# Five lanes instead of six in a four-block transformer stack: slots, banks, pairs and a new order of work

## The chip, the cores and the metric

The kernel runs on one core of one Trainium2 chip. The metric is the device time of one execution in microseconds (us), as the median of several runs; lower is better. A profile is one execution of its own, recorded by the hardware profiler. In it PE is TensorE (matrix products), PEld its loading of weights, DVE is VectorE, ACT is ScalarE, POOL is GpSimd and SP is SyncE, which issues nearly all transfers (DMAs) here.

## What is computed

Thirty-two sequences of 64 tokens with 256 features, all in float32, pass through four blocks one after the other. `ctx` has the same shape and stays as it is.

```python
def stack(x, ctx):                       # both (32, 64, 256)
    x = block0(x, ctx)   # 16 heads of 16; queries from x, keys and values from concat(ctx, x): 128 a sequence
                         # masked softmax, out_w, + x, rmsnorm, gelu(. @ w1) @ w2 (1024 wide), + x
    x = block1(x, ctx)   # layernorm, token shift, five mixes, then a recurrence over the 64 tokens
                         # with a state of 32 heads x 8 x 8, whose start is rows 2..9 of ctx;
                         # group norm, gate, Wo; then a channel mix with fWk, fWr, fWv
    x = block2(x, ctx)   # layernorm, self attention (q, k, v = three parts of w_qkv), layernorm,
                         # cross attention over ctx, layernorm, gelu(. @ w1 + b1) @ w2, each + x
    x = block3(x, ctx)   # cross attention over layernorm(ctx), x + tanh(gate) * out
    return x
```

In the recurrence each head holds a state `s` of 8 x 8; for each token `out = r . (faaaa * k v + s)` and `s = k v + w * s`.

## The kernel before, in words

**Groups, jobs and lanes.** The sequences form NG = 8 groups of GB = 4, so a group is 256 tokens, held as 128 partitions by two tiles of 256 features (token major) or as two chunks of 128 features by 256 tokens (feature major). One block of one group is a job: 32 jobs. A *lane* (class `Lane`, line 388) is a private set of buffers in which one job runs at a time: `SLOTS` slots in SBUF of 2080 bytes a partition (`L.s()`, `L.d()`), a few small tiles, and `BANKS` PSUM banks of 128x512. There are NL = 6 lanes of 10 slots; lanes 0 and 1 have two banks, the other four have one, eight in all. All lanes share the engines.

**The list of jobs.** `JOBS` (line 59) names, in the order in which lanes become free, the block of the next job; `next_job` (1536) gives it the first group that is ready for that block. Each block is a Python generator, and the loop from line 1574 advances the lanes in turn, one `yield` each. Groups pass `x` from one block to the next through DRAM (`load_x`, `store_x`).

**The order of the instructions.** What the loop records is not the order that runs. `order_instructions` (378) takes the recorded instructions, works out what each depends on, and `list_schedule` (283) puts them into one order with a cost of each from `Op.cost` (157): of those that could start, the earliest goes first, and among equals the one of lowest rank. The rank is the place at recording plus an entry of `PUT_BACK` (90), one entry for each RUN = 30 instructions. Each engine then executes its own instructions strictly in that order, and waits on semaphores where it must.

**Products.** `matmul` (516) has two forms. With plain float32 operands it is one instruction (line 520). With *pairs* each operand is a float32r high part and a float32r rest, and the product is three float32r instructions (line 523): high by high, high by rest, rest by high. `split` (509) makes a pair from an activation: a ScalarE copy (512) and a VectorE subtraction (513). `load_w` (501) makes one from a weight: a transfer into a staging buffer, of which there is one (`STAGES`), a ScalarE copy (505) and a VectorE subtraction (506); a pair of weights takes two of the `W_BUFS` = 27 weight buffers, a plain weight one. `SPLIT` says which blocks use pairs: before, blocks 0 and 3. Block 2's cross keys and values are pairs in any case. A projection of one group (`project_T`, 618, or `project`, 632) is four products of 128x256 for each 256 columns of weight, into one bank. In block 2 `SPLIT` decides over q, k and v (lines 1389, 1390, 1399) and the four parts of w1 (1414), and over the split of what the first and the third layernorm give (1450, 1476).

**Attention.** Scores are taken by a quarter of the heads at a time (`r` = 0 to 3), in matmuls of 64 rows by 64 columns of the array: `attention64` (774) for blocks 2 and 3, line 787, and line 987 for block 0; line 888 lays a mask under them where there is one. Below, one `r` is called a head. `side_by_side` (763) takes two such heads at once, on different halves of the array's rows, in lanes with more than one bank, and one at a time in the others. Then `softmax_unit` (731) finds the maximum on VectorE (736), subtracts it (738), transposes on TensorE (744), and exponentiates on ScalarE (745). In block 2 the scores are first masked by VectorE (1438) and GpSimd (1439). Sums over keys (800, 999) and products with the values (810, 1013) use columns of 32.

**Block 1.** The recurrence runs along the tokens by VectorE's scan (1293), 128 scans of 260 columns, between products on VectorE (1290, 1297); line 1303 sums over the state's rows on TensorE. Each job of it makes 16 transfers of 128 KB each from `vd` in DRAM.

**Two places that the change touches besides.** `weights1` puts the initial state of the recurrence into place (lines 1111 to 1125): four transfers of rows of ctx into the staging buffer, and for each eight matmuls with the identity (line 1120), whose weights are every eighth column of the rows, into a bank of lane 0. And block 0 starts by loading ctx and x tiles (line 907), all on SP's queue; the first such pair is lane 0's, group 0, tile 0, transposed by TensorE at line 911. ScalarE's queue issues the constants at the start (539 to 549).

Of the kernel before, what the change touches and what calls it, by code (L numbers as in the profile page):

```python
# [44 lines left out]
P = 128  # L45
B, S, D = 32, 64, 256
NC = D // P
GB = 4
NG = B // GB
W_BUFS = 27  # L50
STAGES = 1
NL = 6
SLOTS = (10, 10, 10, 10, 10, 10)
STAGGER = 4

SPLIT = (0,3)
BANKS = (2, 2, 1, 1, 1, 1)

JOBS = "00010110000111222211233222333333"
GT = GB * S  # L60
TT = GT // P
NH, DH = 16, 16
# [3 lines left out]
HS = 8  # L66
# [21 lines left out]

RUN = 30
PUT_BACK = (  # L90
    -151, -197, 167, -46, 45, -228, -363, -247, 293, 104, -401, -687, -701, -257, -2, 122, -362,
    -546, -151, -305, -598, -113, -406, -253, 285, 87, 144, -352, 182, 97, -397, 471, 223, -176,
    -102, -136, -405, 153, -17, -213, 335, -950, -802, -808, -81, -197, -36, -73, -62, -390, -287,
    -198, -344, -179, 96, 109, -55, -46, 76, 31, -186, 136, -193, 388, -122, -155, -25, -49, 84,
    -346, -135, -279, -555, -592, -190, 1, 46, 55, -5, 34, 220, -102, 175, 263, 161, 365, 177, 333,
    315, 92, 40, 382, 320, 472, 316, 52, -349, -11, -488, -32, -197, -653, -428, -646, -112, -21,
    104, -11, 323, 14, -30, 59, -342, -206, -1207, -1842, -47, -62, -77, -410, 107, 66, 49, 245,
    -243, 50, 105, -347, -77, -279, -21, -179, -201, -751, -308, -188, 134, -60, 2, -472, -574, 174,
    54, -91, -79, -201, 139, -81, -37, 116, -329, 40, -21, -186, 234, 134, 243, 209, -112, -48, 95,
    319, 36, -120, 40, 91, 53, 125, 66, 184, 215, -383, 105, 280, -80, 40, -108, 230, 77, 67, -36,  # L100
    153, 378, -26, 267, 539, 363, 360, 540, -223, 603, -972, -232, -692, 173, 77, 168, -418, -345,
    0, -69, -1239, -1027, -382, -58, -41, 50, -626, 123, 106, -244, 162, -304, 121, 484, 398, 1009,
    438, 401, 299, -29, -187, -274, -49, -69, -90, 65, -55, 280, 46, 837, 722, 85, 335, -61, -90,
    94, -634, 189, -1199, -486, -41, -21, -173, -217, -199, 223, -202, -131, -59, 287, 395, 467,
    423, -358, 136, -59, 32, -226, 109, 72, -389, -543, 228, 248, 513, 404, 120, 266, 46, -340, 312,
    506, -835, -53, 144, -152, 89, -55, 348, 746, 370, -67, -146, 272, -234, -198, 20, 215, 603,
    -20, 161, 1029, 1278, -429, -199, -75, 292, 91, 256, -46, 196, 6, 139, 252, 17, -214, -417, -63,
    -115, -193, -223, -263, -199, 23, 1083, 252, 416, 768, 675, -48, -156, 83, 352, 1157, 140, 134,
    177, 281,
)  # L110
ENGINES = ("PE", "DVE", "Activation", "Pool", "SP")
LATENCY = {"PE": 40, "DVE": 34, "Activation": 33, "Pool": 34}
# [6 lines left out]
class Op:  # L119
# [37 lines left out]
    def cost(self, n, psum, wide):  # L157
        ins, kind = self.ins, self.kind
        self.lock, self.load, self.table = False, 0.0, None
        if kind == "DMACopy":  # L160
            self.ns, steps = 400.0, ins.outs[0].ap
            self.bytes = 4
            for _, m in steps:
                self.bytes *= m
            if len(steps) > 2:
                self.ns = 480.0
        elif self.engine == "PE":
            moving, weights = ins.ins[0], ins.ins[1]
            dt = str(moving.dtype).split(".")[-1]
            cols = 1  # L170
            for _, m in list(moving.ap)[1:]:
                cols *= m
            m = 1
            for _, k in list(weights.ap)[1:]:
                m *= k
            passes = {"float32": 4, "float32r": 1}.get(dt, 1)
            if ins.is_transpose:
                passes = 2
            self.ns = passes * cols / 2.4 + {4: 4, 2: 2}.get(passes, 9 if dt == "float32r" else 2)
            self.load = m * {"float32": 0.6, "float32r": 0.3}.get(dt, 0.2) / (2 if ins.is_transpose else 1)  # L180
            (r, c), (h, w) = ins.tile_position, ins.tile_size
            self.shape = (h, w)
            self.cells = [
                (i, j) for i in range(r // 32, (r + h + 31) // 32) for j in range(c // 32, (c + w) // 32)
            ]
        elif self.engine == "DVE":
            self.ns = {
                "BNStats": 415, "BNStatsAggregate": 165, "StreamTranspose": 190 + 1.02 * n,
                "Reciprocal": 130 + 6.7 * n, "TensorCopy": 80 + n, "TensorReduce": 62 + 1.2 * n,
            }.get(kind, 62 + 1.21 * n)  # L190
            if kind == "TensorTensor":
                self.lock = wide > 1
            elif kind == "TensorScalarPtr":
                if ins.is_tensor_tensor_scan:
                    self.ns, self.lock = 670.0, True
                elif ins.is_scalar_tensor_tensor:
                    self.ns, self.lock = 210 + 1.04 * n, wide > 1
                else:
                    self.ns, self.lock = 140 + 0.95 * n, not psum
        elif self.engine == "Activation":  # L200
            func = str(getattr(ins, "func", "")).split(".")[-1]
            self.table = TABLES.get(func)
            if func == "Exp" and n >= 512:
                self.ns = 597.0
            elif kind == "TensorCopy":
                self.ns = (364.0 if n <= 256 else 590.0) if psum else 100 + 1.02 * n
            else:
                self.ns = 400.0 if n <= 128 else 470.0 if "Gelu" in func else 560.0 if n <= 256 else 680.0
        else:
            self.lock = kind not in ("Memset", "RegisterMove")  # L210
            if kind == "TensorTensor":
                self.ns = 703.0 if n <= 2 else 60 + 2.41 * n
                self.lock = n > 2
            else:
                self.ns = {"Memset": 95 + 0.84 * n, "TensorCopy": 190 + 0.5 * n}.get(kind, 190 + 0.84 * n)
# [209 lines left out]
def kernel(ctx: ExitStack, tc: tile.TileContext, a: dict, out: bass.AP):  # L425
    nc = tc.nc
# [473 lines left out]
    def block0(L, g):  # L900
        mb = key_mask(L, "mask0", g, mybir.dt.int32, 2 * S)
        ct = None
        for i in range(TT):

            cl = tok2(L.d())
            for h, src in enumerate((a["ctx"], a["x"])):
                nc.sync.dma_start(out=cl[:, h], in_=token_major(src, g)[:, i, :])
            ps = L.bank("T").rearrange("p (c h t) -> p c h t", c=NC, h=2)
            for c in range(NC):
                for h in range(2):  # L910
# [152 lines left out]
    def weights1():  # L1063
# [47 lines left out]
        for h in range(2):  # L1111
            ps = lanes[0].bank("T")[:, : NC * HS * B // 2].rearrange("p (t b) -> p t b", b=B)
            for u in range(2):
                st_rows = mk(wpool, [P, NC, D], "stage", STAGES).rearrange("p c n -> p (c n)")
                nc.sync.dma_start(
                    out=st_rows[:B],
                    in_=a["ctx"][:, 2 + 4 * h + 2 * u : 4 + 4 * h + 2 * u, :].rearrange("b s d -> b (s d)"),
                )
                for t in range(HS):
                    nc.tensor.matmul(  # L1120
                        ps[64 * u : 64 * u + 64, t, :],
                        lhsT=st_rows[:B, t : t + (P // 2 - 1) * HS + 1 : HS], rhs=ident[:B, :B],
                        start=True, stop=True,
                    )
            nc.vector.tensor_copy(s0T[:, h], ps)
# [261 lines left out]
    def weights2():  # L1387
        yield
        W["l2_q"] = wload(2, "l2_wqkv")
        W["l2_k"] = wload(2, "l2_wqkv", col0=D)  # L1390
        W["kb2"] = masked_bias("l2_kb", ind)
        W["qb2"] = masked_bias("l2_qb", par)
        W["m1"] = mk(const, [P, S], "m1")
        for j in range(2):
            nc.sync.dma_start(out=W["m1"][j * S : (j + 1) * S, :], in_=a["mask1"][0, 0])
        W["f1"] = mk(const, [P, S], "f1")
        mask_fill(W["f1"], W["m1"])
        yield
        W["l2_v"] = wload(2, "l2_wqkv", col0=2 * D)
        load_row("l2_aob", rows_d)  # L1400
        W["cqb2"] = masked_bias("l2_cqb", par)
        W["ckb2"] = masked_bias("l2_ckb", ind)
        yield
        W["l2_ao"] = mload("o", "l2_wao")
        W["l2_cq"] = mload("c", "l2_wq")
        yield 0
        W["l2_ck"] = load_w("l2_wkv")
        yield 0
        W["l2_cv"] = load_w("l2_wkv", col0=D)
        load_row("l2_cob", rows_d)  # L1410
        load_row("l2_b2")
        W["l2_co"] = mload("o", "l2_wco")
        yield 0
        W["l2_w1"] = [wload(2, "l2_w1", col0=o) for o in range(0, DFF, D)]
        yield 0
        W["l2_w2"] = [mload("h", "l2_w2", row0=o) for o in range(0, DFF, D)]
# [292 lines left out]
```

## Time and profile before

| what | value |
|---|---|
| runs | 1040.76, 1044.8, 1045.53 us; median 1044.8 |
| the profiled execution | 1046.34 us, of which the span from first to last instruction is 1044.6 us |
| mean granted TensorE clock | 0.985 |
| instructions in the trace | 25099 |
| TensorE busy, first 26 us | 17.29 us |
| TensorE busy, 26 to 52 us | 24.90 us |
| TensorE busy, each 100 us from 200 to 1000 | 95.7, 98.6, 96.8, 91.6, 98.3, 100.0, 98.4, 98.3 us |
| TensorE busy, last 45 us | 40.15 us |
| VectorE busy, the same eight stretches | 81.3, 71.7, 88.8, 79.9, 88.0, 64.1, 79.4, 42.3 us |
| HBM traffic over the span | 64 GB/s |

A line of the page's groups reads: source line, engine, operation, output from inputs by tile name, shapes, how many; then busy time in us and the mean of one in ns; then how long the engine stood idle just before them, and what ended that. A float32 product shows as two records, a float32r product or a transpose as one. Records of TensorE overlap their neighbours, so the time that a matmul takes from the stream is read from the distance between starts, in the chain of work or in the timeline.

### The profile page before, as it was taken

The numbers are of one execution on the slowest core, as the hardware profiler recorded it, in microseconds if no ns is written. First come the engines' busy times: TensorE is split into PE (matmuls) and PEld (weight loads), VectorE is DVE, ScalarE is ACT, GpSimd is POOL, SyncE is SP. The second block draws the span as 40 slices with busy tenths as digits, with TensorE's granted clock in tenths as the row PEclk, the third lists the DMA queues.
The fourth block names the chain that finished last, engine by engine and source line by source line (L and its number), as shares of the span: only waits on it lengthen the run. The fifth ranks groups of instructions, "written<-read, shape, count | busy, mean of one in ns | idle before, by whom it ended". The sixth has DMA issues, their size and how long they took to land. (4 is left out here: it accounts for less than half of the span.)

```text
span 1044.6 us, 25099 instructions
## 1 busy us (share of the span) xinstructions
PE 1006.0 (96%) x10012; PEld 826.2 (79%) x10012; DVE 739.1 (71%) x1446; ACT 608.9 (58%) x1241; POOL 350.9 (34%) x501
## 2 busy tenths in 40 slices
PE   6999999999999999999889999999999999999998
PEld 5778878867897786888667878887888788878886
DVE  4662466988867758889878788889655779672157
ACT  6657435454584575546636746565877665654471
POOL 1111033115322414553534665333334543432000
PEclk9999999989999999999969999999999999999999
DMA  6711132411321233233141202222021110010101
GB/s 182 209 36 45 56 94 84 148 52 58 119 65 55 64 101 107 77 102 101 41 132 52 77 24 68 80 71 84 2 82 52 32 42 23 11 42 31 42 21 42
DMA packets 81204, 73.34 MB, mean 70 GB/s; under 512 B 11882, under 2 KB 76864, under 8 KB 81088
## 3 DMA queue, kind: packets, MB, share of 16 engines
q1 hardware_dynamic: 80140, 71.69, 22.4%
q8 instruction: 79, 1.29, 0.5%
q14 instruction: 37, 0.30, 0.1%
q10 hardware_dynamic: 948, 0.05, 0.1%
HBM read 51.77 MB, written 14.68 MB: 64 GB/s over the span
## 5 line engine op out<-in xcount | busy, mean ns | idle before, releaser
L520 PE MATMUL bank<-w,s 128*128 128x256 f32 x1024 | 242.7, 384 | 1.2 <-POOL s L1350 0.6
L520 PEld LDWEIGHTS bank<-w,s 128*128 128x128 f32 x1024 | 190.2, 191 | 30.9 <-issue 2.7
L520 PE MATMUL bank<-s,w 128*128 128x256 f32 x832 | 205.2, 386 | 2.7 <-ACT s L612 2.4
L520 PEld LDWEIGHTS bank<-s,w 128*128 128x128 f32 x832 | 150.5, 191 | 31.1 <-ACT s L612 6.1
L745 ACT ACTIVATE s<-bank 128x512 f32<-128x512 f32 x160 | 92.7, 599 | 102.7 <-PE bank L744 72.2
L523 PE MATMUL bank<-s,w 128*128 128x256 f32 x768 | 120.9, 299 | 0.3
L1439 POOL TENSOR_TENSOR s<-s,f 128x512 f32<-128x512 f32 x64 | 85.5, 1347 | 90.6 <-DVE s L1438 90.4
L523 PEld LDWEIGHTS bank<-s,w 128*128 128x128 f32 x768 | 101.2, 190 | 7.4 <-ACT s L939 1.4
L744 PE MATMUL bank<-ident,s 128*128 128x128 f32 x640 | 97.6, 281 | 5.8 <-DVE s L738 4.6
L744 PEld LDWEIGHTS bank<-ident,s 128*128 128x128 f32 x640 | 74.8, 143 | 25.2 <-issue 12.2
L736 DVE TENSOR_REDUCE mx<-bank 128x4 f32<-128x512 f32 (+1 forms) x96 | 63.7, 681 | 42.1 <-PE bank L987 23.1
L1293 DVE TENSOR_TENSOR_SCAN s<-s,s 128x260 f32<-128x260 f32 x128 | 89.0, 723 | 0.4
L825 ACT ACTIVATE s<-bank,vecs 128x256 f32<-128x256 f32 x128 | 53.4, 470 | 47.5 <-PE bank L520 23.9
L787 PE MATMUL bank<-s,s 64*64 64x128 f32 x1536 | 75.0, 276 | 1.0 <-ACT s L745 0.9
L787 PEld LDWEIGHTS bank<-s,s 64*64 64x64 f32 x1536 | 63.4, 134 | 14.8 <-issue 6.5
L605 ACT ACTIVATE s<-s,shift,rstd 128x256 f32<-128x256 f32 x96 | 52.3, 595 | 38.5 <-DVE shift L602 37.1
L1205 POOL TENSOR_TENSOR s<-s,s 128x512 f32<-128x512 f32 x40 | 52.7, 1324 | 57.9 <-DVE s L1202 22.4
L1060 DVE TENSOR_TENSOR s<-bank,s 128x512 f32<-128x512 f32 x40 | 27.3, 686 | 58.3 <-PE bank L520 58.3
L589 POOL TENSOR_SCALAR rstd<-bnmv 128x2 f32<-128x2 f32 x48 | 12.6, 263 | 156.3 <-DVE bnmv L598 154.8
L612 ACT ACTIVATE s<-bank,vecs 128x256 f32<-128x256 f32 x96 | 48.8, 562 | 26.3 <-PE bank L575 25.7
L738 DVE TENSOR_TENSOR s<-bank,mx 128x512 f32<-128x512 f32 x96 | 63.6, 678 | 0.6
L523 PE MATMUL bank<-w,s 128*128 128x256 f32 x384 | 56.3, 291 | 1.3 <-ACT s L697 0.7
(156 smaller groups left out, 1797.6 us busy)
## 6 DMA issues: line engine op xcount, KB each, us to landing
s<-vd SPq DMA_DIRECT2D x128, 128.0 KB
s<-xd SPq DMA_DIRECT2D x32, 256.0 KB
xd<-s SPq DMA_DIRECT2D x24, 256.0 KB
cxd<-s SPq DMA_DIRECT2D x32, 128.0 KB
s<-s SPq DMA_DIRECT2D x64, 64.0 KB
s<-cxd SPq DMA_DIRECT2D x16, 256.0 KB
w<-in_l_w_dram SPq DMA_DIRECT2D x12, 256.0 KB
s<-in_ctx_dram SPq DMA_DIRECT2D x16, 128.0 KB
```

Source lines behind the costliest of these rows:

```text
L520: nc.tensor.matmul(out, lhsT=lf(l), rhs=rf(r), start=start, stop=stop)
L523: nc.tensor.matmul(out, lhsT=lf(l[u]), rhs=rf(r[v]), start=start and n == 0, stop=stop and n == 2)
L605: nc.scalar.activation(xn[:, i, :], src[:, i, :], AF.Identity, bias=shift[:, i : i + 1], scale=rstd[:, i : i + 1],)
L736: nc.vector.tensor_reduce(mx, sv, AX.X, ALU.max)
L738: nc.vector.tensor_tensor(d.rearrange("p (m n) -> p m n", n=n), sv, mx.unsqueeze(2).to_broadcast([P, m, n]), ALU.subtract,)
L744: nc.tensor.transpose(pt[:, i * P : (i + 1) * P], d[:, i * P : (i + 1) * P], ident)
L745: nc.scalar.activation(d, pt, AF.Exp, scale=scale)
L787: nc.tensor.matmul(sc[64 * b : 64 * b + 64, o : o + P], lhsT=q(r, c, seq), rhs=k(r, c, seq), start=not begun, stop=not begun or (i, c) == ...
L825: each(lambda c, ps: nc.scalar.activation(h[:, c, :], ps, AF.Gelu_apprx_tanh, bias=chunk8(b1, NC * o + c))),
L1205: nc.gpsimd.tensor_tensor(xf, xf, xa, ALU.add)
L1293: nc.vector.tensor_tensor_scan(f, wT[:, c].rearrange("p b s -> p (b s)"), f, 0.0, ALU.mult, ALU.add)
L1439: nc.gpsimd.tensor_tensor(sv, sv, f, ALU.add)
```

## The change

Lanes: five of eleven slots (55 in all, where there were 60), three of them with two banks and two with one (still eight). Block 2 joins `SPLIT`, and the weight buffers become 33. `JOBS` and `PUT_BACK` are new lists; the costs that the planner uses change in one figure, the fixed part of a float32r product. The state rows are first copied by ScalarE into a slot of lane 0 such that the eight sets of weights are contiguous. The first pair of ctx and x loads goes to ScalarE's queue. In `weights2` one `yield` moves by a line.

By the jobs' lists, lanes 0 to 5 before ran the following block.group jobs: 0.0 1.2 1.5 1.7 2.7; 0.1 0.4 1.4 1.6 2.6 3.7; 0.2 0.5 2.0 2.4 3.6; 1.0 0.6 2.1 3.0 3.2 3.4; 0.3 0.7 2.3 2.5; 1.1 1.3 2.2 3.1 3.3 3.5. After, lanes 0 to 4 run 0.0 0.4 0.5 1.5 1.7 2.6 3.7; 0.1 1.1 0.7 2.1 2.3 2.7; 0.2 1.2 1.3 1.6 2.4 3.3 3.6; 1.0 1.4 2.0 3.0 3.1 3.2 3.5; 0.3 0.6 2.2 2.5 3.4.

```diff
-W_BUFS = 27
+W_BUFS = 33
 STAGES = 1
-NL = 6
-SLOTS = (10, 10, 10, 10, 10, 10)
+NL = 5
+SLOTS = (11, 11, 11, 11, 11)
 STAGGER = 4
 
-SPLIT = (0,3)
-BANKS = (2, 2, 1, 1, 1, 1)
+SPLIT = (0, 2, 3)
+BANKS = (2, 2, 2, 1, 1)
 
-JOBS = "00010110000111222211233222333333"
+JOBS = "00010011010011222112322322333333"
...
 PUT_BACK = (
-    -151, -197, 167, -46, 45, -228, -363, -247, 293, 104, -401, -687, -701, -257, -2, 122, -362,
...
+    -1234, -1569, -1480, -2741, -2282, -2700, -2430, -1690, -2575, -718, -1857, -964, -1477, -1589,
...
-            self.ns = passes * cols / 2.4 + {4: 4, 2: 2}.get(passes, 9 if dt == "float32r" else 2)
+            self.ns = passes * cols / 2.4 + {4: 4, 2: 2}.get(passes, 12 if dt == "float32r" else 2)
...
             for h, src in enumerate((a["ctx"], a["x"])):
-                nc.sync.dma_start(out=cl[:, h], in_=token_major(src, g)[:, i, :])
+                queue = nc.scalar if (g, i) == (0, 0) else nc.sync
+                queue.dma_start(out=cl[:, h], in_=token_major(src, g)[:, i, :])
...
+                by_t = lanes[0].d()[:B].rearrange("p (t m) -> p t m", t=HS)
+                nc.scalar.copy(by_t, st_rows[:B].rearrange("p (m t) -> p t m", t=HS))
                 for t in range(HS):
                     nc.tensor.matmul(
-                        ps[64 * u : 64 * u + 64, t, :],
-                        lhsT=st_rows[:B, t : t + (P // 2 - 1) * HS + 1 : HS], rhs=ident[:B, :B],
+                        ps[64 * u : 64 * u + 64, t, :], lhsT=by_t[:, t, :], rhs=ident[:B, :B],
...
         W["l2_ao"] = mload("o", "l2_wao")
+        yield 0
         W["l2_cq"] = mload("c", "l2_wq")
-        yield 0
         W["l2_ck"] = load_w("l2_wkv")
```

## The prediction

> **What bounds the kernel now.** I read the page's first part, then its costliest groups, the chain of work, and the stretches where TensorE loses time. First part:
>
> ```profile
> PE 1006.0 (96%) x10012; PEld 826.2 (79%) x10012; DVE 739.1 (71%) x1446; ACT 608.9 (58%) x1241; POOL 350.9 (34%) x501
> ```
>
> TensorE is busy 96% of 1044.6 us and VectorE 71%, so a change counts by what it does to TensorE's stream and to its gaps. The groups (records, busy us, mean ns, idle before) show its two kinds of 128x256 product. A float32 product leaves two records, so 1024 + 832 records are 928 products; a float32r product leaves one, and a product in pairs takes three.
>
> ```profile
> L520 PE MATMUL bank<-w,s 128*128 128x256 f32 x1024 | 242.7, 384 | 1.2 <-POOL s L1350 0.6
> ...
> L520 PE MATMUL bank<-s,w 128*128 128x256 f32 x832 | 205.2, 386 | 2.7 <-ACT s L612 2.4
> ...
> L523 PE MATMUL bank<-s,w 128*128 128x256 f32 x768 | 120.9, 299 | 0.3
> ```
>
> The mean (384, 299) holds a pipelined tail, so prices must come from starts. The chain in order of time (start, us, what, records) gives clean runs:
>
> ```profile
> 671.18 11.22 PE bank L520 x52
> ```
>
> ```profile
> 885.73 2.86 PE bank L523 x24
> ```
>
> 11.22 us over 26 products is 431 ns for a float32 product; 2.86 over 24 is 119 ns a record, 357 ns for a product in pairs.
>
> The idle time is about 39 us: 6.1 before the first transpose, about 4 after the last matmul, the rest in short gaps but one, which VectorE leaves when it is behind. The timeline around it, then two stretches (busy us by engine, then the granted clock):
>
> ```profile
> 523.16 0.92 PE L744 MATMUL bank<-ident,s 128*128 128x128 f32 x4 [3.08 <-DVE s L738]
> ```
>
> ```profile
> 520.00:525.00 5.00, 1.75 (x10) 1.26 (x8) 5.00 (x9) 2.20 (x3) 1.65 (x2) 0.84 0.00 0
> 525.00:530.00 5.00, 4.28 (x30) 2.48 (x28) 2.89 (x5) 2.11 (x4) 1.32 (x2) 0.50 0.01 3
> ```
>
> VectorE is busy for 5.00 of 5 us while TensorE has 1.75; then TensorE runs at half clock, until 540.4. Such an episode costs its gap, 3.1 us, and half of 17.0 us: 11.6 us. There is one in this trace; three other half-clock stretches (134.2 to 137.6, 219.6 to 226.4, 502.9 to 506.3) cost 6.8 us together.
>
> **Block 2 in pairs.** q, k, v and the four parts of w1 change from float32 to pairs: 7 projections x 4 products x 8 groups = 224 products, 448 records out and 672 in. By clean runs that is 224 x (431 - 357) = 16.6 us less. But a projection that starts after a wait lays its first float32r records further apart. From every start to the next over the whole trace, the 1855 L520 intervals sum to 405.9 us and the 1152 L523 ones to 162.0: 438 and 422 ns a product, 3.6 us less in all. Most of these 56 projections start after a wait, but then run 12 records; I take 10 us between the ends (-16.6 to -3.6).
>
> The price elsewhere: 16 splits (L512 620 ns on ScalarE, L513 711 on VectorE, from SBUF) and 7 weight splits (about 650 and 680): 14.5 us of ScalarE and 16.2 of VectorE, three table loads more by the order (1.28 us each). ScalarE at 58% and VectorE at 71% have room on average, and other lanes' products cover the 1.33 us by which each split delays its projection. Uncovered it would cost 16 x 1.33 = 21 us. In the stretches 400 to 500 and 600 to 700, VectorE is busy 88.8 and 88.0 us of 100: there the cover is thin.
>
> The weight-load rows speak against this edit. PEld is busy 190.2 us for 1024 L520 records, 186 ns each and 372 a product, and 101.2 us for 768 L523 records, 132 each and 395 for three. The Trainium skill (Perfetto Trace Analysis, Identifying the Most-Contended Engine) says that TensorE is to be judged by weight-load time rather than matmul time. By that the pairs would cost 224 x 23 ns = 5 us instead of saving. The starts decide for me: they count both.
>
> **Two banks in three lanes of five.** A head's scores (L787, 16 records) are four quadrants' work; with two banks two heads run side by side. Three rows of the timeline:
>
> ```profile
> 1011.10 1.04 PE L787 MATMUL bank<-s,s 64*64 64x128 f32 x32
> 1012.07 0.65 PE L575 MATMUL bank<-ident,s 128*128 128x128 f32 x4
> ...
> 1013.35 1.06 PE L787 MATMUL bank<-s,s 64*64 64x128 f32 x16
> 1014.34 0.48 PE L520 MATMUL bank<-s,w 128*128 128x256 f32 x1
> ```
>
> Two heads take 0.97 us to the next start, one alone 0.99. By the jobs' lanes, 20 of 96 such heads have two banks before and 52 after: 32 x 0.5 = 16 us less. For block 0 (L987), 24 of 64 heads before, 48 after; over the trace a head costs 0.61 us with two banks and 0.85 with one: 24 x 0.24 = 5.7 less. Against it stands that the old order already lays heads of different one-bank lanes beside each other: at 817.45 the chain has 96 L787 records, six heads, in 3.84 us, 0.64 a head. Walking both orders and counting steps in which a quadrant holds one matmul, L787 needs 265 before and 281 after (about 215 ns each, half of a product twice as wide), L987 92 and 84 (430 ns), L888 66 and 63 (215 ns): net 0.6 us less. So -22 to 0; I take -3, near the order, since it is this order that runs.
>
> **Five lanes, eleven slots, jobs and ranks.** Nothing is computed more or less, but each lane's work must come sooner. I walked both orders again: for each first reading of a tile, the TensorE work (by these rows) that stands between it and the matmul whose bank the tile came from, less the durations of what lies between on the other engines. The margin is negative at 27 places before and 37 after, under 1 us at 149 and 152. In the trace the 27 lost 13.3 us beyond the products' own price, and the next 122 lost 3.7; at the same loss by size of the margin, the new order loses 13.4 and 3.7. So I take 0. It knows nothing of queues on VectorE: one episode less would be -11.6, one more +11.6. The 33 buffers hold the seven more lo halves; the swapped yield moves one load on SP's queue, hidden.
>
> **State rows in order.** The 64 records of L1120 have strided weights, load for 212 ns each, and start 120 ns apart. Contiguous ones, by the transposes (L744, 128 columns, 109 ns) halved to 64 columns, would be 55 to 60 apart: 64 x 60 = 3.8 us. Ends: 64 x 93 = 5.9 less, if they went at 27 ns like side-by-side heads, and 2.8 more, if the rate stays and the four new copies (about 0.65 us each on ScalarE, of a group of four loads, with one more slot of lane 0) are not covered by other lanes. I take -4.
>
> **First loads on ScalarE's queue.** Lane 0's ctx load is issued at 2.48 and x at 4.23, and PE starts at 6.09 and 6.98. On ScalarE's queue they stand behind three and then two more issues of 0.4 to 1.2 us: about 2.1 and 5.0, so x lands 0.8 later. But lane 1's pair is issued on SP at about 3 us instead of 8.56, and its transposes need not wait until 12.15. TensorE idles 2.6 us between 6.09 and 26, so -2.6 to +1; I take -1.
>
> **The sum.** -10 - 3 + 0 - 4 - 1 = -18. The profiled execution took 1046.3 us (span 1044.6), 1.5 above the median of the runs, 1044.8; from that median 1027 us.
>
> **The rivals.**
> All ends at once (0.16): -16.6 - 22 - 5.9 - 2.6 = -47, so 998 us. For it: each end is a row of this trace. Against it: the walk gives the quadrants almost nothing.
> The pairs are hidden by waits (0.17): they save 3.6, state rows 4, and the 11.4 us of new splits in block 2 fall into stretches where VectorE is the bound: +3.8, so 1048.6. For it: VectorE's 88%. Against it: TensorE loses only 3.2 and 1.8 us of idle in those two stretches.
> Five lanes run dry (0.15): with one lane less, VectorE's queue leaves gaps like that at 520, each with its half clock, 11.6 us. It decides from two more episodes (-18 + 23 = +5, 1050); with three it is 1062. For it: no lane is left to fill in, and ten more negative margins. Against it: nearly equal loss by margin, and two banks let a lane work on two heads.
> The Trainium skill (TensorE: Matmul & The Clock Gate, Part 1) has the clock fall only after an idle window of about 3.4 us, so only gaps that long would cost; three of the four stretches here follow gaps of at most 1.3 us. The trace does not bear the threshold out.
>
> **Chances.** The forecast case (1003 to 1039) has 0.52. Within 0.5%, about what a measurement of this kernel can tell from no change, is 1039.6 to 1050.0: the second rival. Faster 0.68, same 0.17, slower 0.15. The range is 1000 to 1054: some 0.06 lies below it and 0.10 above.
>
> **What would show it.** TensorE's records rise by 224 to 10236, VectorE's instructions by 23. Right: the new block 2 products at 119 ns in runs, the state rows' records near 60 ns apart, busy plus idle of TensorE falling together, idle near 40 us. Wrong: float32r records of block 2 mostly 200 ns and more apart; gaps above 1 us that end on VectorE; more than 31 us at half clock; the last 45 us, where fewer lanes share the end, with more idle than the 5 us of now.

## The result, and the profile after

| | before | after |
|---|---|---|
| median of seven runs (range) | 1044.17 us (1040.76 to 1048.12) | 1049.04 us (1043.65 to 1052.26) |
| ratio | | 1.0048, interval 1.0025 to 1.0070 |
| the profiled execution, its span | 1046.34, 1044.6 us | 1052.26, 1050.5 us |
| TensorE busy | 1006.0 us | 986.6 us |
| TensorE idle up to its last matmul | 34.6 us | 59.6 us |
| of that, gaps over 1 us | 6 | 15 |
| time at half clock, up to the last matmul | 30.7 us | 27.3 us |

The change makes the kernel about 5 us slower, where 18 less were forecast. The idle time is worked out from the trace: the time between the end of one TensorE record and the start of the next, where no record runs. Busy and idle together rise by 5.6 us, and the span by 5.9. Each profile is one execution, and that of the kernel after is the slowest of its seven.

The first part of the page of the kernel after, then its two kinds of product among the groups (records, busy us, mean ns, idle before):

```profile
PE 986.6 (94%) x10236; PEld 820.3 (78%) x10236; DVE 765.6 (73%) x1469; ACT 630.6 (60%) x1271; POOL 362.6 (35%) x501
```

```profile
L522 PE MATMUL bank<-w,s 128*128 128x256 f32 x960 | 227.6, 383 | 2.6 <-DVE s L817 1.8
L525 PE MATMUL bank<-s,w 128*128 128x256 f32 x1344 | 203.0, 296 | 9.8 <-ACT s L827 3.9
```

L522 and L525 are L520 and L523 of before. The records rise by 224 and VectorE's instructions by 23, as forecast. TensorE's busy time falls by 19.4 us, near the 17 that the forecast's pairs, banks and state rows add to; by an estimate, 1.7 us of it is the 3.4 us less at half clock. But the float32r products now have 9.8 us of idle ahead of them, where the group shown of before had 0.3. Runs of the chain in order of time hold the old prices, 118 ns for a float32r record and 432 for a float32 product (26 records, 13 products):

```profile
799.85 2.72 PE bank L525 x23
802.57 5.61 PE bank L522 x26
```

So in runs without waits the products cost what was foreseen, and what TensorE saves it then waits away. The view of waits on TensorE says for whom (us in total, times, longest). Of the kernel after:

```profile
PE bank L914 <- DMA s<-in_ctx_dram: 10.9, 4, 6.5
PE bank L746 <- DVE s L740: 6.2, 9, 2.1
PE bank L577 <- DVE s L1342: 4.5, 2, 2.9
PE bank L525 <- ACT s L827: 3.9, 5, 1.7
PE bank L577 <- ACT s L607: 3.4, 9, 1.1
PE bank L525 <- DVE shift L604: 2.7, 1, 2.7
PE bank L1201 <- DMA s<-s: 2.5, 3, 1.3
PE bank L914 <- DMA s<-in_x_dram: 2.3, 1, 2.3
```

and of the kernel before:

```profile
PE bank L911 <- DMA s<-in_ctx_dram: 7.1, 2, 6.1
PE bank L744 <- DVE s L738: 4.6, 5, 3.1
PE bank L575 <- ACT s L605: 4.6, 12, 0.9
PE bank L520 <- ACT s L612: 2.4, 2, 1.3
```

Summed over all rows of this view, the waits on VectorE go from 8.8 to 21.6 us, on transfers from 8.0 to 16.1, on ScalarE from 15.5 to 18.3, on GpSimd from 0.6 to 2.0. There is no one new wait; there are many, of many kinds, and in every stretch of 100 us from 100 to 800 but 500 to 600 TensorE is less busy than before.

### The profile page after: what moved, and what is told of

The parts are those of the page before. It is cut to its first block, busy times and chain, and to the rows that moved or that the text cites. A ratio compares the mean times of both kernels' runs of the same rounds, so it can differ in the third digit from the quotient of the medians.

```text
span 1050.5 us, 25590 instructions
## 1 busy us (share of the span) xinstructions
PE 986.6 (94%) x10236; PEld 820.3 (78%) x10236; DVE 765.6 (73%) x1469; ACT 630.6 (60%) x1271; POOL 362.6 (35%) x501
## 5 line engine op out<-in xcount | busy, mean ns | idle before, releaser
L522 PE MATMUL bank<-w,s 128*128 128x256 f32 x960 | 227.6, 383 | 2.6 <-DVE s L817 1.8
L525 PE MATMUL bank<-s,w 128*128 128x256 f32 x1344 | 203.0, 296 | 9.8 <-ACT s L827 3.9
L522 PEld LDWEIGHTS bank<-w,s 128*128 128x128 f32 x960 | 176.1, 190 | 29.5 <-issue 2.8
L525 PEld LDWEIGHTS bank<-s,w 128*128 128x128 f32 x1344 | 174.0, 191 | 22.1 <-ACT s L827 6.7
L1443 POOL TENSOR_TENSOR s<-s,f 128x512 f32<-128x512 f32 x64 | 87.8, 1379 | 104.7 <-DVE s L1442 98.2
L522 PE MATMUL bank<-s,w 128*128 128x256 f32 x448 | 113.4, 394 | 3.3 <-POOL s L1209 1.0
L746 PE MATMUL bank<-ident,s 128*128 128x128 f32 x640 | 94.8, 276 | 8.0 <-DVE s L740 6.2
L522 PEld LDWEIGHTS bank<-s,w 128*128 128x128 f32 x448 | 82.3, 194 | 20.9 <-POOL s L1209 2.2
L1297 DVE TENSOR_TENSOR_SCAN s<-s,s 128x260 f32<-128x260 f32 x128 | 94.0, 755 | 0.2
L746 PEld LDWEIGHTS bank<-ident,s 128*128 128x128 f32 x640 | 72.4, 140 | 24.7 <-issue 10.4
L525 PE MATMUL bank<-w,s 128*128 128x256 f32 x480 | 72.1, 291 | 0.3 <-ACT s L699 0.3
L591 POOL TENSOR_SCALAR rstd<-bnmv 128x2 f32<-128x2 f32 x48 | 16.2, 338 | 146.3 <-DVE bnmv L600 143.8
L525 PEld LDWEIGHTS bank<-w,s 128*128 128x128 f32 x480 | 62.1, 189 | 2.8 <-ACT s L699 1.3
L614 ACT ACTIVATE s<-bank,vecs 128x256 f32<-128x256 f32 x96 | 49.5, 566 | 20.5 <-PE bank L577 20.1
```

The lines of the kernel that those rows point to most:

```text
L522: nc.tensor.matmul(out, lhsT=lf(l), rhs=rf(r), start=start, stop=stop)
L525: nc.tensor.matmul(out, lhsT=lf(l[u]), rhs=rf(r[v]), start=start and n == 0, stop=stop and n == 2)
L614: each(lambda c, ps: nc.scalar.activation(t[:, c, :], ps, AF.Identity, bias=vec(b, c), scale=vec(w, c))),
L746: nc.tensor.transpose(pt[:, i * P : (i + 1) * P], d[:, i * P : (i + 1) * P], ident)
L1297: nc.vector.tensor_tensor_scan(f, wT[:, c].rearrange("p b s -> p (b s)"), f, 0.0, ALU.mult, ALU.add)
L1443: nc.gpsimd.tensor_tensor(sv, sv, f, ALU.add)
```

## The experiments

In the table, idle, gaps over 1 us and half clock (us) are of the profiled execution of each kernel, up to its last matmul; ratios are to runs of the kernel before on the same chip.

| kernel | median us | ratio (interval) | TensorE busy | idle | gaps | half clock |
|---|---|---|---|---|---|---|
| e_start | 1047.1 | 1.0029 (1.0009 to 1.0049) | 988.7 | 58.0 | 15 | 30.7 |
| e_plain2 | 1103.8 | 1.0549 (1.0513 to 1.0584) | 1019.2 | 80.2 | 26 | 54.6 |
| e_six_w1 | 1088.6 | 1.0413 (1.0363 to 1.0462) | 1019.9 | 64.1 | 17 | 47.8 |
| e_banks | 1119.7 | 1.0718 (1.0697 to 1.0740) | 1026.6 | 88.9 | 20 | 75.1 |
| k_start | 1051.5 | 1.0056 (1.0029 to 1.0084) | 990.6 | 57.5 | 14 | 37.5 |
| k_nosub | 1046.2 | 1.0025 (0.9996 to 1.0054) | 984.0 | 55.8 | 13 | 23.9 |
| k_prod | 1058.3 | 1.0132 (1.0091 to 1.0173) | 998.2 | 53.5 | 12 | 17.1 |
| k_rows | 1041.2 | 0.9962 (0.9947 to 0.9976) | 996.8 | 37.9 | 8 | 20.5 |
| t6_s1 | 1048.0 | 1.0028 (1.0003 to 1.0054) | 997.2 | 45.2 | 11 | 20.5 |
| t5_s1 | 1045.3 | 1.0002 (0.9983 to 1.0021) | 990.7 | 49.5 | 15 | 10.2 |
| t5p_s1 | 1049.2 | 1.0042 (1.0016 to 1.0067) | 988.0 | 60.2 | 23 | 41.0 |
| t5p_s2 | 1043.8 | 0.9984 (0.9962 to 1.0007) | 975.9 | 59.5 | 15 | 6.8 |
| k_scanA | 1042.9 | 0.9970 (0.9954 to 0.9985) | 989.8 | 56.2 | 14 | 34.1 |
| k_scanB | 1038.4 | 0.9927 (0.9898 to 0.9956) | 994.5 | 33.2 | 7 | 6.8 |
| k_gap | 1041.7 | 0.9966 (0.9953 to 0.9980) | 997.9 | 38.9 | 9 | 23.9 |
| t5_s2 | 1065.1 | 1.0191 (1.0148 to 1.0233) | 998.5 | 59.6 | 13 | 44.4 |
| t6_s2 | 1063.2 | 1.0181 (1.0141 to 1.0222) | 1008.8 | 54.0 | 14 | 27.3 |

### First: one part at a time, ordered again with the old ranks

Theory A was that one lane less leaves TensorE without work to fill in; its rivals were the first loads, the pairs with their splits, and the third two-bank lane. In these four kernels one part is changed, the list of ranks stays (in two of them its places carried over where the number of instructions differs), and `list_schedule` makes a new order.

e_start: the first loads go back to SP's queue.

```diff
-                queue = nc.scalar if (g, i) == (0, 0) else nc.sync
+                queue = nc.sync
```

> Only the first pair of ctx and x loads goes back to SP's queue; all else is the changed kernel. In its trace the x half lands at 11.2 us, where it stood behind 3 us of issues on ScalarE's queue, against 7.0 in the kernel before, and TensorE is busy 15.1 of the first 26 us against 17.3. If the queue move is part of the loss, the transposes of x start before 8.5 us, the first 26 us hold 1.5 to 3 us more work, and the time falls by 1.5 to 3 us, to 1046 to 1047.5. If the start is made up later (TensorE waits less afterwards), the time is within 1 us of 1049.

e_plain2: the kernel after, with block 2 in plain products.

```diff
-SPLIT = (0, 2, 3)
+SPLIT = (0, 3)
```

> The changed kernel with block 2 in plain float32 again, five lanes; every other instruction keeps its rank. Theory A, one lane less leaves TensorE short of ready work: the idle time stays near 60 us and the products come back, 10 to 17 us, so 1059 to 1066. Theory B, the splits that the pairs need fill VectorE's queue and lengthen the chains, and that is the new idle: idle falls to some 40 us, and the time to 1040 to 1047.

e_six_w1: the kernel before, with the four parts of w1 of block 2 in pairs (`wload` makes a pair where it is given "2w1").

```diff
-        W["l2_w1"] = [wload(2, "l2_w1", col0=o) for o in range(0, DFF, D)]
+        W["l2_w1"] = [wload("2w1", "l2_w1", col0=o) for o in range(0, DFF, D)]
...
-        hT = layernorm_T(L, x, 1e-5, "l2_ln3_s", "l2_ln3_b", pair=2 in SPLIT)
+        hT = layernorm_T(L, x, 1e-5, "l2_ln3_s", "l2_ln3_b", pair=True)
```

> The kernel before, six lanes, with pairs for the four parts of w1 of block 2 alone (128 of the 224 products, 8 of the 16 activation splits, 4 of the 7 weight splits); other instructions keep their ranks. Theory A: the pairs save what they save in the changed kernel's stream, 2 to 9 us, so 1035 to 1042. Theory B: no gain or a loss, 1044 to 1050.

e_banks: the kernel after, with one bank in lane 2; there that lane also yields once for two heads, so that the turns of the lanes stay as they were.

```diff
-BANKS = (2, 2, 2, 1, 1)
+BANKS = (2, 2, 1, 1, 1)
...
-            yield
+            if L.n != 2 or rs[0] % 2:
+                yield
```

> The changed kernel with one bank in lane 2, so that 20 heads of 64 columns and 8 tiles' heads of block 0 there go one after the other; the rest as it is. If the second bank is worth what two heads side by side save alone, the time rises by 8 to 11 us, to 1057 to 1060. If, as the walk of the orders has it, heads of other lanes fill the other half of the array anyway, it stays within 3 us of 1049.

e_start comes out 2 us below after, with intervals that overlap. The other three are 44 to 75 us slower than before, with 64 to 89 us of idle and up to 75 at half clock. All three lie far outside what either theory expected. I take this as the list's doing: over a slightly different program the same list gave a poor order. For the pairs the next part bears that out, where single products in a kept order cost 9 us and not 55; for the second bank no run in a kept order exists. So these three answer nothing on lanes, pairs or banks. From here on either the order itself is kept, or a list is searched anew for each program.

### Second: one part at a time, in the order as it stands

In these kernels the order of the instructions of after (or, for k_rows, of before) is written out, and only what the edit names differs.

k_start: after, with the same edit as e_start.

> The changed kernel with its order of instructions written out, so that nothing is planned anew, and only the first ctx and x loads issued on SP's queue at the same places. If the queue is what makes the start later, x lands by 8.5 us instead of 11.2 and the time falls by 2 to 3 us against the changed kernel's 1049. If something else holds TensorE there (the larger loads ahead of them), within 1 us.

k_nosub: after, without the 16 subtractions for the splits of block 2's activations.

```diff
+        if pair and b in ("l2_ln1_b", "l2_ln3_b"):
+            hi = feat2(L.s(F32R))
+            nc.scalar.copy(hi, t)
...
+            return hi, hi
         return split(L, t) if pair else t
```

> The changed kernel's order kept; of block 2's sixteen activation splits the VectorE subtraction is left out, and the high part stands in for the rest, so the product's low-order part is not computed. VectorE has 11.4 us less to do. Theory B (the splits in VectorE's queue are the new idle time): the time falls by 8 to 11 us, to 1038 to 1041, and TensorE's waits for VectorE fall from about 22 us to 12 or less. Theory A (with five lanes any delay on VectorE is uncovered, wherever it comes from): it falls by 4 us at most.

k_prod: after, with one float32 product in place of each triple in block 2; the splits stay. `WIDE` holds the weights that `wload` loads for block 2.

```diff
+        if any(m is l or m is r for m in WIDE):
+            nc.tensor.matmul(
+                out, lhsT=lf(l[0]).bitcast(F32), rhs=rf(r[0]).bitcast(F32), start=start, stop=stop
+            )
...
             return
         for n, (u, v) in enumerate(((0, 0), (0, 1), (1, 0))):
```

> The changed kernel's order kept, all splits kept; only the products of block 2's pairs are one float32 instruction of the two high parts instead of three float32r ones, so the low-order parts are not computed. If the pairs save in this stream what clean runs say (74 ns each), the time rises by 13 to 17 us, to 1062 to 1066. By the mean distance of all starts (16 ns each) it rises by 3 to 4, to 1053. If the saved time only turns into waiting for other engines, it stays at 1049 within 2.

k_rows: before, with the state rows put in order by ScalarE (here within the staging buffer) and nothing else.

```diff
+                by_t = st_rows[B : 2 * B].rearrange("p (t m) -> p t m", t=HS)
+                nc.scalar.copy(by_t, st_rows[:B].rearrange("p (m t) -> p t m", t=HS))
...
-                        lhsT=st_rows[:B, t : t + (P // 2 - 1) * HS + 1 : HS], rhs=ident[:B, :B],
+                        lhsT=by_t[:, t, :], rhs=ident[B : 2 * B, B : 2 * B],
```

> The kernel before, its order kept, with the state rows alone put in order: four ScalarE copies within the staging buffer ahead of the 32 matmuls of the initial state, no slot of a lane. If the term of the prediction holds, the 64 records start about 58 ns apart instead of 120 and the time falls by 3 to 4 us, to 1040.5 to 1041.5 where the kernel before has 1044.5. If the copies are not covered, within 1 us of the kernel before.

The queue of the first loads is not the loss: back on SP's queue the time is 1051.5, beside 1049.0. The subtractions are at most a small part, 2.9 us by medians, with intervals that overlap. The products in pairs do pay: without them the time is 9.3 us longer (8.8 by the ratios, with some 5 either way), TensorE's busy time 11.6 us, and idle 6.1 us less, since the longer products cover some of it. The profile of k_prod had 10.2 us less at half clock; with half of that put back its products are 16.7 us dearer by this estimate, which is what clean runs said (16.6). And the state rows pay: k_rows is 3.4 us below before, by the ratio 0.24 to 0.53%. The two rows of that line (records, busy us, mean ns), before and k_rows, in one fence each:

```profile
L1120 PE MATMUL bank<-ident,stage 32*64 32x32 f32 x64 | 8.4, 280 | 0.0
```

```profile
L1278 PE MATMUL bank<-ident,stage 32*64 32x32 f32 x64 | 4.5, 219 | 0.3 <-ACT stage L1275 0.3
```

Their starts lie 58 ns apart instead of 120 (medians). In the kernel after they do so too, but there one of the four copies comes late: TensorE waits 1.06 us for it at 171.5, and 3.4 us at half clock follow. So after has less of this gain than k_rows. k_rows is the fastest kernel of this study that computes everything, and below both given ones.

### Third: a list searched anew for each program

Here each program gets a list of ranks that starts from zeros and is searched with the same effort, by the kernel's own planner with the costs of after: six lanes as before (t6), five as after with block 2 plain (t5), and the whole of after (t5p), two seeds each. All have the state rows and the first loads of after. Short of the lists the edits are:

```diff
# t6: before's W_BUFS, NL, SLOTS, BANKS, JOBS; t5, t5p: after's
-SPLIT = (0, 2, 3)
+SPLIT = (0, 3)          # t6 and t5
 PUT_BACK = (...)        # new in each
```

t6_s1:

> Six lanes of ten slots with the banks and jobs of the kernel before and block 2 in plain float32, with the two start edits of the change (state rows, first loads), and a list of ranks searched anew from zeros with the kernel's own planner: as long a search as for the next three. Theory A (one lane less leaves TensorE dry): this one has the least idle time of the four, 40 us or so. Theory C (how well a list fits the chip decides, not the lanes): all four differ by the luck of their lists, two lists of the same program by 10 us and more; every one of them is above 1049.

t5_s1:

> The same with the five lanes, banks and jobs of the change, block 2 still in plain float32. Theory A: slower than six lanes by 10 us or more, by idle time. Theory C: within the spread of two lists of one program.

t5p_s1:

> The changed kernel whole (five lanes, block 2 in pairs) with a list searched anew in the same way. The products save 9 us by the run with single products and the splits cost some 3, so 3 to 9 us below the five lanes with plain block 2, if lists are equally good. Theory A: still above six lanes' time.

t5p_s2:

> The same program once more with a list from another start of the same search. Its distance from the one before is the spread that a list alone makes: Theory C says 5 to 25 us, Theory A under 5.

t6_s2:

> Six lanes with the banks and jobs of before, block 2 in plain products; a second list of the same effort. If lanes matter (theory A): at least 6 us below the five-lane ones of the same seed. If not: between 1042 and 1053, within the spread of lists of the five-lane ones.

t5_s2:

> Five lanes with the banks, slots and jobs of after, block 2 in plain products; a second list of ranks, found with the same effort from another seed. If the spread among lists (5.4 us between two lists of the kernel after) is what decides: between 1040 and 1051. If pairs pay as the prediction says: 4 us or more above the mean of the two lists with pairs, 1046.5.

With the first seed five lanes are 2.8 us below six, with the second 1.9 above. Theory A had five lanes 10 us or more above with the first and 6 or more with the second, and there is no sign of that. But with two lists each, which lie 15 and 20 us apart, an effect of several us either way can't be excluded. Of pairs (t5p against t5), the first seed says 3.9 us slower, the second 21.3 faster. The lists alone differ by amounts like these: 5.4 us between two lists of t5p, 19.8 of t5, 15.2 of t6, though the two lists of each order the same work. And k_rows, which has the lanes and jobs of t6 and the order of before, is 7 and 22 us below the two t6. So before came with a better list than this effort finds, and which list a program gets can be worth more than the whole change. Theory C missed too: three of the first four kernels are below its 1049, and t6_s2 and t5_s2 are 10 and 14 us above the upper ends expected.

Of idle, t6 has 45 and 54 us, t5 49.5 and 59.6, t5p 60.2 and 59.5. No fresh list comes near before's 35, and five lanes have 4 to 6 us more than six with each seed. All three lists for the program of after, the given one included, leave 59.5 to 60.2 us. t5p_s2 is faster than after by less time at half clock (6.8 against 27.3 us), not by less idle. So part of the new idle may belong to the program itself, whatever its list: its shorter products leave less to lay beside the same chains. No run here puts the pairs into the order of before, which could tell.

### Fourth: is it a queue on VectorE, or the order?

Two theories were left. Q: the new idle is waiting in VectorE's queue. P: it is where the order puts chains that nothing covers, whichever engines they run through. A large cut of VectorE's work, the same in both orders, is to tell them apart.

```diff
                     nc.vector.tensor_tensor_scan(
-                        f, wT[:, c].rearrange("p b s -> p (b s)"), f, 0.0, ALU.mult, ALU.add
+                        f[:, : S + 1], wT[:, c, 0], f[:, : S + 1], 0.0, ALU.mult, ALU.add
                     )
                 st = st[:, :, :, :S]
-                nc.vector.tensor_tensor(st, st, per_t(rT[:, c, :]), ALU.mult)
+                nc.vector.tensor_tensor(
+                    st[:, :, :1], st[:, :, :1], per_t(rT[:, c, :])[:, :, :1], ALU.mult
+                )
```

k_scanA:

> The kernel after with its own order of instructions kept, and in the recurrence of block 1 the scan takes one of the four sequences (65 columns of 260) and the product with r one of four; so the output leaves out the recurrence of three sequences in four. Some 90 us of VectorE's 766 go, and nothing else. Theory Q (TensorE's 25 us of extra idle are waits in VectorE's queue): idle falls from 60 by 20 or more, to within 6 us of the same cut made in the kernel before, and the time stands at least 10 us below that one's, for TensorE has 19 us less to do. Theory P (the idle is where the order itself puts work that nothing can cover, behind ScalarE, transfers and chains as much as behind VectorE): idle stays 12 us or more above that of the same cut in the kernel before, and the two times lie within 7 us of each other.

k_scanB:

> The same cut in the kernel before, its order kept; the output leaves out the same part. Theory Q: its idle of 35 us falls little (8 or less), since its waits on VectorE are 9 us in all, and the time by at most 15 (the episode at 520 with its half clock). Theory P: the idle falls about as much as in the kernel after under the cut.

The first part of the page of k_scanA, then of k_scanB:

```profile
PE 989.8 (94%) x10236; PEld 823.8 (78%) x10236; DVE 684.2 (65%) x1469; ACT 629.3 (60%) x1271; POOL 344.4 (33%) x501
```

```profile
PE 994.5 (96%) x10012; PEld 819.2 (79%) x10012; DVE 657.8 (64%) x1446; ACT 609.0 (59%) x1241; POOL 335.8 (33%) x501
```

VectorE loses 81 us in both (90 had been expected), and TensorE's idle falls by 3.4 us in the order of after and 1.4 in that of before: 56.2 against 33.2. By their ratios the times fall by 0.8 and 0.7%, and the order of after stays 4.5 us above, where Q had it 10 or more below. The profile of k_scanA is the slowest of its twelve executions, 9.1 us above their median; even if all of that were idle time, idle would have fallen by 12.5 us, and Q asked for 20. Q falls. Nor does the profile of k_scanB stand for its median, it is 5.0 us below, so the 23 us between the two idle times are rough. The waits on VectorE hardly shrink (21.6 to 19.5 in all), so little of them was queueing behind the work that is left out; queueing behind VectorE's other 684 us isn't tested. The largest gap shows what such a wait can be made of. Timeline of the kernel after (start, us, engine, what):

```profile
254.82 1.16 PE L1322 MATMUL bank<-center,s 128*128 128x128 f32 x8
...
255.82 1.89 PE L522 MATMUL bank<-w,s 128*128 128x256 f32 x8
256.02 0.60 ACT L1334 ACTIVATE s<-bank 128x512 f32<-128x512 f32 x1 [2.11 <-PE bank L1322]
256.63 1.28 ACT L1339 ACT_TABLE_LOAD   x1
256.65 1.02 DVE L1336 TENSOR_REDUCE gvar<-s 128x64 f32<-128x512 f32 x1
...
257.93 0.35 ACT L1339 ACTIVATE gvar<-gvar,eps 128x64 f32<-128x64 f32 x1
258.18 0.68 DVE L1032 TENSOR_TENSOR s<-bank,s 128x512 f32<-128x512 f32 x1
258.78 0.54 DVE L1340 RECIPROCAL gvar<-gvar 128x64 f32<-128x64 f32 x1
...
259.24 0.64 DVE L1297 TENSOR_TENSOR_SCAN s<-s,s 128x260 f32<-128x260 f32 x1
...
259.79 0.67 DVE L1342 TENSOR_TENSOR s<-bank,gvar 128x512 f32<-128x512 f32 x1
...
260.61 0.97 PE L577 MATMUL bank<-ident,s 128*128 128x128 f32 x4 [2.90 <-DVE s L1342]
```

This is block 1's group norm: square, sum, root, reciprocal, product, over two engines, with a table load in it. From the last L1322 product (255.98) to the transposes at 260.61 it takes 4.6 us, and the order has laid only 1.9 us of products beside it. VectorE delays two steps behind work of other lanes, about 0.5 us each (L1340 behind L1032, L1342 behind the scan L1297). In k_scanA the same place:

```profile
256.48 1.16 PE L1479 MATMUL bank<-center,s 128*128 128x128 f32 x8
...
257.47 1.89 PE L677 MATMUL bank<-w,s 128*128 128x256 f32 x8
...
258.29 1.28 ACT L1496 ACT_TABLE_LOAD   x1
...
260.03 0.54 DVE L1497 RECIPROCAL gvar<-gvar 128x64 f32<-128x64 f32 x1
...
260.64 0.67 DVE L1499 TENSOR_TENSOR s<-bank,gvar 128x512 f32<-128x512 f32 x1
...
261.45 0.63 PE L732 MATMUL bank<-ident,s 128*128 128x128 f32 x4 [2.09 <-DVE s L1499]
```

Most of the delays behind other lanes is gone, and 2.09 of 2.90 us stay: from 257.64, where the L1479 products end, the chain alone takes 3.8 us, twice what stands beside it.

k_gap asks what one gap costs. It is k_rows with one place of the order changed, at the gap that both k_rows (3.07 us, at 518.6) and before (3.08, at 523.2) have. The six places are those of lane 2's subtraction (VectorE), its four transposes and its exponential (ScalarE).

```diff
+MOVE = {4976: -11.5, 4977: -7.5, 4978: -8.4, 4979: -9.3, 4980: -10.2, 4981: -9.5}; LATER = {}
...
-        keyed.append((turn[place] + LATER.get(ins.name, 0), n, ins))
+        keyed.append((turn[place] + LATER.get(ins.name, 0) + MOVE.get(place, 0), n, ins))
```

> The kernel before with the state rows in order and its order kept but for one place: in the queue of lane 2's softmax at the gap near 520 us one VectorE subtraction stands ahead of two reductions of other lanes, and its four transposes and its exponential stand ahead of lane 5's. Nothing is computed more or less. If an episode costs its gap and half of what follows at half clock, as the prediction priced it (11.6 us): the gap falls from 3.1 to about 1.2 us, no half clock follows, and the time falls by 6 to 10 us from 1041.2. If the wait only moves to the next transposes: at most 2 us less.

The timeline of TensorE in k_gap, then two of its stretches (busy us by engine, then the granted clock):

```profile
518.82 0.63 PE L899 MATMUL bank<-ident,s 128*128 128x128 f32 x4 [2.26 <-DVE s L893]
521.35 1.09 PE L899 MATMUL bank<-ident,s 128*128 128x128 f32 x4 [1.90 <-DVE s L893]
```

```profile
520.00:525.00 5.00, 2.92 (x20) 2.28 (x20) 3.68 (x7) 2.48 (x3) 0.20 (x1) 0.50 0.01 3
525.00:530.00 5.00, 5.00 (x31) 2.61 (x30) 2.61 (x5) 0.60 (x1) 1.66 (x1) 0.50 0.00 0
```

The gap did not go, it split in two of 2.26 and 1.90 us, and the half clock behind it lasts 13.7 us as in k_rows. The time is the same, 1041.7 beside 1041.2. Here a wait taken from one place of the order came back at the next; since no run removed the gap, what it costs with its half clock stays open.

## Why the prediction was wrong, point by point

| step of the prediction | forecast | measured |
|---|---|---|
| pairs in block 2 | -10 (-16.6 to -3.6) | -9.3, some 5 either way (k_prod) |
| their splits | 0 | 2.9 for the subtractions, an interval that reaches 0 (k_nosub) |
| two banks in three lanes | -3 | not to be isolated |
| lanes, slots, jobs and ranks | 0 | about +18, some 5 either way: what is left over, with banks and splits in it |
| state rows | -4 | -3.4 (k_rows); its copies took 1.1 us each, where 0.65 was forecast |
| first loads | -1 | within the uncertainty of 0 (k_start, e_start) |

**The step that failed** is "Five lanes, eleven slots, jobs and ranks", where it says "So I take 0". By the medians 1049.0 - 1044.2 = +4.9; pairs and state rows gave -12.7, so +17.6 is left for the order with its lanes and banks and the splits together. TensorE's own rows say the same: 19.4 us less busy, 25.0 more idle. The walk over margins took the loss for a function of the margin's size, fixed by the trace of before. By the same walk over the trace of after (its working is in no view shown here), the negative margins lost 10.7 us, less than the 13.4 forecast, but those from 0 to 1000 ns lost 11.4 where 3.7 were forecast, and those from 1000 to 4000 ns, which the prediction left out, lost 11.1 where in before they lost 2.8. So the loss by size of margin didn't carry over from one order to the other. Why not is argued, not shown: a margin priced by the durations of a chain's links leaves out what stands between them, like the table load and the other lanes' instructions in the gap at 260.6 us.

**The text named its blind spot and mistook it.** "It knows nothing of queues on VectorE" pointed to load; k_scanA's profile has 81 us less load on VectorE and 3.4 us less idle. At the one gap that was followed, it is the chain's length against the work laid beside it; for the other gaps that isn't shown.

**Why this order waits more** stays open in part. Five lanes show no loss in time that stands out from the spread of lists (t5 against t6, 2.8 us below and 1.9 above), though they have 4 to 6 us more idle. Lists of equal effort differ by 5 to 20 us for one program, and before's list stands 7 to 22 us below fresh ones for its lanes, so a less good list alone could be the 18 us. Against that stands that all three lists for the program of after leave 60 us of idle. The jobs, the slots, the third two-bank lane and the planner's new cost were not tested one by one. Whether a longer searched list for the program of after would get below before's time stays open too; t5p_s2 at 1043.8, level with before, is the best seen of it.

**What was right.** The -10 for the pairs was picked between two ends 13 us apart, so that it came within 1 us is partly luck; the price in clean runs held. The price of the state rows was right by its reason, 58 ns between starts. Of the text's own signs of being wrong, float32r records mostly 200 ns apart did not come (118 ns in the middle), nor a worse end: the last 45 us have 4.8 us without TensorE, as before.

**Two rivals had nearly the right time for the wrong reason.** "The pairs are hidden by waits" (1048.6) says that they save 3.6 us; they save 9.3. "Five lanes run dry" (1050) has episodes in VectorE's queue, each with 8.5 us lost to half clock; but time at half clock fell, from 30.7 to 27.3 us, and 81 us less load on VectorE brought little back. Its sign that decides, gaps over 1 us that end on VectorE, is there in part: of 15, seven end on VectorE (two of six in before), five on transfers and three on ScalarE.

**On the pairs** the Trainium skill (Perfetto Trace Analysis, Identifying the Most-Contended Engine) takes weight-load time, beside the share of peak FLOPs, and not matmul time as the measure of TensorE's distance to its roofline. k_prod and after differ in just these products: weight-load time is 818.7 us with float32 products and 820.3 with pairs, a rise of 1.6, while the time falls by 9.3. The distances between starts had the sign right: 224 float32 products of k_prod take 103.2 us from start to start, 461 ns each; the float32r records of after take 255.7 us and the 1152 that k_prod keeps 159.8, so block 2's 672 take 95.9 us, 428 ns a product.

**On the first loads** the prediction had x land 0.8 us later; its transposes start 4.2 us later (6.98 in the kernel before). Rows of the timeline of after:

```profile
2.72 2.96 ACTq L551 DMA_DIRECT2D halfT<-in_half_dram  x2
5.72 2.01 ACTq L910 DMA_DIRECT2D s<-in_x_dram  x1
11.21 1.11 PE L914 MATMUL bank<-ident,s 128*128 128x128 f32 x4 [2.33 <-DMA s<-in_x_dram]
```

Two issues of ScalarE's queue took 2.96 us and the next 2.01, where 0.4 to 1.2 each had been read from before. What was right is that the other lanes' loads come earlier, and over the whole kernel it is no loss that can be measured.

## What to carry to other kernels

Where a planner writes the order, price a change in two parts: what its instructions save, which distances between starts bounded here, and what the new order does with it, which was off by 18 us here; before believing a gain or a loss, keep the order and change the part, or compare several lists of each program. A list of ranks belongs to one program; the same ranks over another came out 4 to 7% slower here. And when an engine is busy 96% of the time, part of what its work is shortened by can come back as waiting (6.1 of 11.6 us between k_prod and after); look for the chain that takes longer than what stands beside it, not for the busiest helper.

## What the runs showed of the hardware that was not expected

The half clock comes in whole steps up to the last matmul: 3.4, 6.8, 10.2, 13.7, 17.1 or 20.5 us in all these traces. Within a trace its starts lie whole steps apart too: 172.0, 260.7 and 489.4 us in the kernel after, 26 and 67 steps of 3.413 us. It followed single gaps as short as 1.1 us (at 656.5 in the kernel after), while one of 2.12 us (at 221.1) left the clock at full. In the kernel before it came at 134.2 us with no gap over 0.2 us in the ten us ahead, right behind 16 of the state rows' small matmuls. The Trainium skill (TensorE: Matmul & The Clock Gate, Part 1) has a free-running window of about 3.4 us; the steps agree with it, and a fall only after an idle window doesn't, since in the traces of before and after no gap but the first is that long.

The same gap doesn't lead to the same stretch: 3.08 us in before came with 17.1 us at half clock, 3.07 in k_rows with 13.7 that began 1.0 us before the gap's end, 2.68 in k_scanB with 6.8. So executions of one kernel, which lie 2 to 13 us apart here, can't be told to a microsecond from one profile.

Weights with a stride of eight columns made the state rows' matmuls start 120 ns apart, contiguous ones 58, which is the price that the prediction had taken from halved transposes.
